# One exponential over three PSUM banks for a pair of key tiles in a graph attention

## The chip, the cores and the metric

The kernel runs on one core of a Trainium2 chip. The metric is the device time of one execution in microseconds (us); lower is better. The engines work side by side, each through its own list of instructions in order, and wait for each other through semaphores: PE multiplies matrices into PSUM (eight banks of 512 float32 columns on 128 partitions), ACT (ScalarE) computes functions such as the exponential, DVE (VectorE) and POOL (GpSimd) work element by element, SP starts DMA transfers. POOL has no part in PSUM here: what it reads lies in SBUF.

## The reference

Four graph layers are applied to 3327 nodes with 128 features, each as `x = x + layer(relu(layernorm(x)))`. The change lies in the second, an attention of 128 heads whose feature dimension per head is 8:

```python
q = (x @ Wq.T).reshape(d, n, h)          # d = 128 heads, n = 3327 nodes, h = 8
k = (x @ Wk.T).reshape(d, n, h)
v = (x @ Wv.T).reshape(d, n, h)
a = jnp.einsum('dnh,dmh->dnm', q, k) * scale
a = a + spatial_encoding + edge_encoding  # both are the adjacency matrix: + 2 * adj
a = jax.nn.softmax(a, axis=2)
out = jnp.einsum('dnm,dmh->dnh', a, v)
```

So for each head, 3327 x 3327 scores are made, twice the adjacency (0 or 2) is added to each, all are exponentiated, and the result weighs the values. The kernel takes no maximum off (another path, not run for this input, does) and gets the sum of each row from a ninth value column of ones.

## The kernel before

**Tiling.** Queries go along the columns in chunks of QW = 476 (seven chunks, the last of 471, computed as 472), keys along the partitions in T = 26 tiles of 128. Heads go in groups of four (32 groups): each head's small contraction takes one of the four 32-row groups of PE, so that four heads' score matmuls can run side by side. The loop is `steps = [(c, g, t) ...]`, chunk by chunk, group by group, key tile by key tile: 7 x 32 x 26 = 5824 steps, 2912 pairs of an even and an odd step. A pair shares one tile `p8` of eight planes of 476 columns in SBUF (`p_pool`, three buffers), four planes for each step.

**Three ways to add 2 * adj.** Each of a step's four heads has a letter in `WAYS`:

- D: PE writes the score into a PSUM tile `early` (one bank, four buffers); DVE adds `a2` (twice the adjacency) on the way to `p8` (L552). The exponential comes later.
- I: PE writes the score into a PSUM tile `late` and adds `a2` itself with a second matmul, of `two_i` (the identity) with `a2` (L550). ACT takes the exponential from PSUM to `p8` (L553).
- G: PE writes the score into `late`, ACT takes its exponential, and POOL multiplies it by `e`, the exponential of `a2` (L555).

The even step has DDDI, the odd one DDIG. `PLACES` puts the five D planes of a pair at 0 to 4, so that one ACTIVATE of 5 x 476 = 2380 columns, in place, does all of them (L557, after the odd step), and the three late ones at 5, 6 and 7:

```python
WAYS = ("DDDI", "DDIG")
PLACES = ((0, 1, 2, 5), (3, 4, 6, 7))
```

**PSUM.** `acc` takes one bank, `early` four, `late1` (even step) one, `late2` (odd step) two: all eight. `late1` and `late2` have one buffer each, so the next pair's late scores can't be written until ACT has read this pair's.

**Order.** All engines' orders are as written (`tc.manual_schedule`). `scores` issues for one step: late scores and then early scores on PE (L547), the identity matmul (L550), DVE's adds (L552), the exponential of the late tile (L553, 476 columns in the even step, 952 in the odd), POOL's multiply (L555, odd), the exponential of 2380 columns (L557, odd). After it `weigh` is called for the step `ahead = 4` steps earlier, that is two pairs: four matmuls of the values (9 columns each, on four column groups) with the planes of `p8` into `acc` (L564). They are in float32 and show in the trace as two MATMULs each. At the last key tile DVE copies `acc` out (L573) and four DMAs store it. Around these, by step number: `load_heads` loads the next group's keys, queries and values at t = 4, `key_pair` converts keys on POOL (L419) from t = 13, `Parting` splits later groups' keys and queries in the first chunk, adjacency tiles of the next chunk are loaded, doubled (L272) and stored, and in a chunk's last group ACT makes the next chunk's `e` (L347).

Of the kernel before, what the change touches and what calls it, by code (L numbers as in the profile page):

```python
# [8 lines left out]
F32 = mybir.dt.float32  # L9
# [6 lines left out]
AF = mybir.ActivationFunctionType  # L16
ALU = mybir.AluOpType
# [4 lines left out]
P = 128  # L22
N = 3327
D = 128
# [7 lines left out]
QW = 476  # L32
# [5 lines left out]
def rows_of(t):  # L38
    return P if t < T - 1 else P - 1
# [15 lines left out]
def kernel(  # L55
# [23 lines left out]
    nc = tc.nc  # L79
# [90 lines left out]
    def load_rows(dst, src, t, col0, w):  # L170

        def part(p0, p1):
            nc.sync.dma_start(dst[p0:p1, :w], dram(src, (p0 * T + t) * N + col0, [[T * N, p1 - p0], [1, w]]))

        if t < T - 1:
            part(0, P)
        else:
            part(0, 112)
            part(112, P - 1)
# [85 lines left out]
    def doubled(pool, a, t, w):  # L265
        kp = rows_of(t)
        a2 = pool.tile([P, QW], BF16, name="a2")
        if w % 2:
            nc.gpsimd.memset(a2[:, w : w + 1], 0.0)
        if kp < P:  # L270
            nc.gpsimd.memset(a2[96:P], 0.0)
        nc.gpsimd.tensor_scalar(a2[:kp, :w], a, 2.0, None, op0=ALU.mult)  # L272
        return a2
# [67 lines left out]
    def even(c):  # L341
        w = q_chunks[c][1]
        return w + w % 2

    def exp_of(a2, c):
        e = e_pool.tile([P, QW], F32, name="e")
        nc.scalar.activation(e[:, : even(c)], a2[:, : even(c)], AF.Exp)  # L347
        return e
# [65 lines left out]
    def key_pair(heads):  # L414

        k_in, _, _, pairs = heads
        t = 2 * len(pairs)
        k = kq.tile([P, 2, P], F32R, name="k", bufs=T)
        nc.gpsimd.tensor_copy(k, slots(k_in)[:, t : t + 2, :])  # L419
        pairs.append(k)  # L420

    with tc.tile_pool(name="l1", bufs=1) as pool, tc.tile_pool(name="l1_ps", bufs=3, space=PSUM) as ps:
# [21 lines left out]
        early = []  # L444
# [60 lines left out]
    WAYS = ("DDDI", "DDIG")  # L505
    PLACES = ((0, 1, 2, 5), (3, 4, 6, 7))
    two_i = const.tile([P, P], BF16, name="two_i")
# [9 lines left out]
    ahead = 4  # L517
    adj_pools.append(ctx_at.enter_context(tc.tile_pool(name="at_adj1", bufs=T)))
    with tc.tile_pool(name="at_in", bufs=1) as a_pool, tc.tile_pool(name="at_p", bufs=3) as p_pool, tc.tile_pool(
        name="at_ps", bufs=1, space=PSUM  # L520
    ) as ps:
        acc = ps.tile([P, 512], F32, name="acc")
        nc.vector.memset(acc, 0.0)

        def load_adj(c, t):

            q0, w = q_chunks[c]
            a = a_pool.tile([P, QW], F32, name="a_in", bufs=1)
            load_rows(a, adjT, t, q0, w)
            return a, t, w  # L530

        def store_adj(c, t, a2):
            q0, w = q_chunks[c]
            nc.sync.dma_start(adj16[t][:, q0 : q0 + w], a2[:, :w])

        def scores(step, heads, a2, e_a, p8):
            c, _, t = step
            we = even(c)
            _, q4, _, pairs = heads
            ways, places = WAYS[t % 2], PLACES[t % 2]  # L540
            n_d = ways.count("D")
            late = ps.tile([P, 4 - n_d, 512], F32, name=f"late{4 - n_d}")
            early = [ps.tile([P, 512], F32, name="early", bufs=4) for _ in range(n_d)]
            for i in (*range(n_d, 4), *range(n_d)):
                r = slice(32 * i, 32 * i + 32)
                sp = early[i] if i < n_d else late[:, i - n_d]
                nc.tensor.matmul(sp[:, :we], pairs[t // 2][r, t % 2, :], q4[r, :we], start=True, stop=ways[i] != "I")  # L547
            for i in range(4):
                if ways[i] == "I":
                    nc.tensor.matmul(late[:, i - n_d, :we], two_i, a2[:, :we], start=False, stop=True)  # L550
            for i in range(n_d):
                nc.vector.tensor_tensor(p8[:, places[i], :we], early[i][:, :we], a2[:, :we], op=ALU.add)  # L552
            nc.scalar.activation(p8[:, places[n_d] : places[3] + 1, :we], late[:, :, :we], AF.Exp)  # L553
            if ways[3] == "G":
                nc.gpsimd.tensor_tensor(p8[:, places[3], :we], p8[:, places[3], :we], e_a[:, :we], op=ALU.mult)  # L555
            if t % 2:
                nc.scalar.activation(p8[:, :5, :we], p8[:, :5, :we], AF.Exp)  # L557

        def weigh(step, v4, p8):
            c, g, t = step  # L560
            q0, w = q_chunks[c]
            kp = rows_of(t)
            for i in range(4):
                nc.tensor.matmul(  # L564
                    acc[32 * i : 32 * i + EA, :w],
                    v4[:kp, i, t, :],
                    p8[:kp, PLACES[t % 2][i], :w],
                    start=(t == 0),
                    stop=(t == T - 1),
                )  # L570
            if t == T - 1:
                o4 = a_pool.tile([P, QW], F32, name="o4")
                nc.vector.tensor_copy(o4[: 96 + EA, :w], acc[: 96 + EA, :w])  # L573
                for i in range(4):
                    n0 = (4 * g + i) * N + q0
                    nc.sync.dma_start(ot[:, n0 : n0 + w], o4[32 * i : 32 * i + EA, :w])

        with tc.manual_schedule(engines=engines):
            groups = [(c, g) for c in range(len(q_chunks)) for g in range(n_groups)]
            steps = [(c, g, t) for c, g in groups for t in range(T)]  # L580
            heads = first
            a_t, a_next = a_first, []
            e_t, e_next = e_first, []
            to_store = [(0, t, a2) for t, a2 in enumerate(a_t)]
            begun = {}
            for j, step in enumerate(steps):
                c, g, t = step
                n = c * n_groups + g + 1
                more = n < len(groups)
                if t == 0 and j:  # L590
                    heads = coming
                    if g == 0:
                        a_t, a_next = a_next, []
                        e_t, e_next = e_next, []
                if t % 2 == 0:
                    p8 = p_pool.tile([P, 8, QW], F32, name="p8")
                scores(step, heads, a_t[t], e_t[t // 2], p8)
                begun[j] = (step, heads[2], p8)
                if j >= ahead:
                    weigh(*begun.pop(j - ahead))  # L600
                if t == min(4, T // 2) and more:
                    coming = load_heads(*groups[n])
                if c == 0 and g + 2 < n_groups:
                    if t == 0:
                        parting = ahead_part
                    for due in range(t, t + 1 if t < T - 1 else max(T, 16)):
                        parting.at(due)
                        if due == 15 and g + 3 < n_groups:
                            ahead_part = Parting(g + 3)
                            ahead_part.load(0)  # L610
                            ahead_part.load(1)

                if t >= T // 2 and more:
                    key_pair(coming)
                if t == min(6, T // 2) and c + 1 < len(q_chunks):
                    for _ in range(min(len(to_store), 1 + T // n_groups)):
                        store_adj(*to_store.pop(0))
                    a_in = [load_adj(c + 1, i) for i in range(len(a_next), T * (g + 1) // n_groups)]
                if t == max(T - 4, 3) and c + 1 < len(q_chunks):
                    for a, i, w in a_in:  # L620
                        a_next.append(doubled(adj_pools[(c + 1) % 2], a[: rows_of(i), :w], i, w))
                        to_store.append((c + 1, i, a_next[-1]))
                if t % 2 and g == n_groups - 1 and c + 1 < len(q_chunks):
                    e_next.append(exp_of(a_next[t], c + 1))
            for j in range(len(steps) - ahead, len(steps)):
                weigh(*begun.pop(j))
            for a in to_store:
                store_adj(*a)
# [372 lines left out]
    with tc.For_i(0, n_once, 1):  # L1001
# [5 lines left out]
        with tc.tile_pool(name="sh", bufs=2) as pool, tc.tile_pool(name="sh_ps", bufs=2, space=PSUM) as ps:  # L1007
            with tc.For_i(0, NH, 1) as hd:
# [5 lines left out]
                for t in range(T):  # L1014
# [4 lines left out]
                    for half, (h0, hw) in enumerate(chunks(N, 2048)):  # L1019
                        sp = ps.tile([P, 2048], F32, name="sp")  # L1020
# [9 lines left out]
        with tc.tile_pool(name="gb", bufs=2) as pool, tc.tile_pool(name="gb_ps", bufs=2, space=PSUM) as ps, tc.tile_pool(  # L1030
            name="gb_acc", bufs=1, space=PSUM
# [3 lines left out]
            with tc.For_i(0, NH // 4, 1) as g:  # L1035
# [8 lines left out]
                for q0, w in chunks(N, QW):  # L1044
                    q4 = pool.tile([P, QW], F32, name="gq4")
                    for i in range(4):
                        nc.sync.dma_start(q4[32 * i : 32 * i + EA, :w], qf[:, bass.ds(g * (4 * N) + i * N + q0, w)])
                    for t in range(T):
# [4 lines left out]
                        for i in range(4):  # L1053
                            r = slice(32 * i, 32 * i + EA)
                            sp = ps.tile([P, 512], F32, name="gsp")
# [3 lines left out]
                        for i in range(4):  # L1059
                            r = slice(32 * i, 32 * i + EA)  # L1060
# [49 lines left out]
```

## Time and profile before

| | us |
|---|---|
| median of 3 runs | 11191.26 (11190.45 to 11191.84) |
| profiled execution | 11195.14 |
| its span on the core | 11193.4 |
| PE busy, of the stretch 580 to 10480 us | 9781.47 of 9900 |
| ACT busy, same stretch | 9891.59 |
| DVE busy, same stretch | 8530.47 |
| POOL busy, same stretch | 5812.99 |

The stretch from 580 to 10480 us is the attention; the granted PE clock in it is 1.00. The page's groups read: line, engine, operation, output<-inputs with partitions x elements and type, count | total busy us, mean ns of one | idle time of the engine just before them, and what ended most of it. "(+1 forms)" means that instructions of another shape are in the same group: L553 mixes 476 and 952 columns. Records of one engine can overlap, since the next instruction begins while the last one's results are on their way; PE's records start at the true time, but their ends are modelled. In the timeline each row is a start, the time from the first start to the last end of the instructions merged in it, engine, line, operation, count, and in brackets the idle time before and what ended it. PEld are weight loads.

### The profile page before, as it was taken

The numbers are of one execution on the slowest core, as the hardware profiler recorded it, in microseconds if no ns is written. First come the engines' busy times: TensorE is split into PE (matmuls) and PEld (weight loads), VectorE is DVE, ScalarE is ACT, GpSimd is POOL, SyncE is SP. The second block draws the span as 40 slices with busy tenths as digits, with TensorE's granted clock in tenths as the row PEclk, the third lists the DMA queues.
The fourth block names the chain that finished last, engine by engine and source line by source line (L and its number), as shares of the span: only waits on it lengthen the run. The fifth ranks groups of instructions, "written<-read, shape, count | busy, mean of one in ns | idle before, by whom it ended". The sixth has DMA issues, their size and how long they took to land. (4 is left out here: it accounts for less than half of the span.)

```text
span 11193.4 us, 209350 instructions
## 1 busy us (share of the span) xinstructions
PE 10850.5 (97%) x79530; PEld 3005.9 (27%) x79530; DVE 9343.1 (83%) x15429; ACT 10199.3 (91%) x9152; POOL 6016.3 (54%) x6964
## 2 busy tenths in 40 slices
PE   9899999999999999999999999999999999999996
PEld 4322222222222222222222222222222222222453
DVE  8588888888888888888888888888888888888656
ACT  0399999999999999999999999999999999999522
POOL 0277777555555555555555555555555555555203
PEclk9899999999999999999999999999999999999998
DMA  7755554333333333333333333333333332333432
GB/s 264 238 129 120 123 127 109 65 64 64 68 64 62 67 66 63 68 65 61 68 66 63 66 66 61 67 66 61 66 66 61 66 63 55 61 58 58 135 113 97
DMA packets 417541, 942.25 MB, mean 84 GB/s; under 512 B 67936, under 2 KB 345937, under 8 KB 380940
## 3 DMA queue, kind: packets, MB, share of 16 engines
q1 hardware_dynamic: 412762, 918.98, 37.4%
q8 instruction: 627, 10.27, 0.4%
q0 software_dynamic: 3760, 9.78, 0.3%
q14 instruction: 392, 3.21, 0.1%
HBM read 788.78 MB, written 139.71 MB: 83 GB/s over the span
## 5 line engine op out<-in xcount | busy, mean ns | idle before, releaser
L552 DVE TENSOR_TENSOR p<-early,a 128x476 f32<-128x476 f32 (+1 forms) x14560 | 8426.4, 646 | 1369.4 <-PE early L547 1297.5
L557 ACT ACTIVATE p<-p 128x2380 f32<-128x2380 f32 (+1 forms) x2912 | 7568.4, 2599 | 0.4
L564 PE MATMUL acc<-p,v 128*9 128x476 f32 (+1 forms) x46592 | 5748.5, 564 | 15.3 <-ACT p L557 1.4
L553 ACT ACTIVATE p<-late 128x476 f32<-128x476 f32 (+1 forms) x5824 | 5315.4, 1175 | 13.8 <-DMA q<-qt 10.2
L555 POOL TENSOR_TENSOR p<-p,e 128x476 f32<-128x476 f32 (+1 forms) x2912 | 3528.1, 1212 | 3204.3 <-ACT p L553 2998.6
L547 PE MATMUL late<-q,k 32*128 32x476 f32 (+1 forms) x8736 | 2798.2, 478 | 99.5 <-ACT p L553 39.7
L547 PE MATMUL early<-q,k 32*128 32x476 f32 (+1 forms) x14560 | 2843.6, 478 | 9.4 <-DVE p L552 9.4
L419 POOL CAST k<-k_in 128x256 fp32r<-128x256 f32 x2912 | 1936.5, 697 | 886.4 <-DMA k_in<-kt 339.4
L547 PEld LDWEIGHTS late<-q,k 32*128 32x128 f32 x8736 | 1065.4, 181 | 4890.4 <-ACT p L553 4186.2
L550 PE MATMUL late<-a,two_i 128*128 128x476 bf16 (+1 forms) x5824 | 2180.8, 374 | 0.0
L547 PEld LDWEIGHTS early<-q,k 32*128 32x128 f32 x14560 | 1113.0, 181 | 9.9 <-DVE p L552 9.9
L564 PEld LDWEIGHTS acc<-p,v 128*9 128x9 f32 x46592 | 695.2, 88 | 1272.6 <-issue 1185.8
L550 PEld LDWEIGHTS <-two_i 128*128 128x128 bf16 x5824 | 556.2, 96 | 1329.0 <-issue 1329.0
L189 ACT COPY agg<-agg_ps 128x512 f32<-128x512 f32 x15 | 8.2, 591 | 485.5 <-PE agg_ps L204 290.6
L230 PE MATMUL agg_ps<-a,part 128*128 128x512 bf16 (+1 forms) x1092 | 227.0, 369 | 4.3 <-ACT agg L928 3.2
L272 POOL TENSOR_SCALAR a<-a_in 128x476 bf16<-128x476 f32 (+2 forms) x156 | 221.1, 1417 | 0.5
L272 POOL TENSOR_SCALAR a<-a 128x476 bf16<-128x476 f32 (+1 forms) x26 | 36.4, 1400 | 288.1 <-DMA a<-in_adjT_dram 288.1
L923 PE MATMUL sp<-yT,hT 128*128 128x512 f32 (+1 forms) x364 | 170.7, 610 | 12.3 <-ACT agg L928 6.4
L204 PE MATMUL agg_ps<-a,h 128*128 128x512 f32 (+2 forms) x364 | 148.2, 570 | 26.2 <-DVE h L164 26.2
L573 DVE COPY o<-acc 105x476 f32<-105x476 f32 (+1 forms) x224 | 144.5, 645 | 4.6 <-PE acc L564 4.6
L204 PE MATMUL agg_ps<-a,x 128*128 128x512 f32 (+2 forms) x364 | 145.3, 562 | 0.6 <-ACT x L318 0.6
L230 PEld LDWEIGHTS <-part 128*128 128x128 f16 x1092 | 108.6, 99 | 117.7 <-issue 10.3
(236 smaller groups left out, 2592.0 us busy)
## 6 DMA issues: line engine op xcount, KB each, us to landing
k_in<-kt SPq DMA_DIRECT2D x1792, 207.9 KB
v<-vd SPq DMA_DIRECT2D x896, 117.0 KB
a<-in_adjT_dram SPq DMA_DIRECT2D x50, 1663.5 KB
a<-adj SPq DMA_DIRECT2D x78, 831.8 KB
q<-qt SPq DMA_DIRECT2D x1536, 29.8 KB
a_in<-in_adjT_dram SPq DMA_DIRECT2D x125, 238.0 KB
adj<-a SPq DMA_DIRECT2D x156, 119.0 KB
vd<-v_st SPq DMA_DIRECT2D x25, 576.0 KB
```

The lines of the kernel that those rows point to most:

```text
L204: nc.tensor.matmul(acc[c][:, :w], lhs[:kp, t, :], a[:kp, c0 : c0 + w], start=(t == 0), stop=(t == T - 1))
L230: nc.tensor.matmul(acc[c][:, :w], part[:, t, :], a[:, c0 : c0 + w], start=(t == 0 and i == 0), stop=(t == T - 1 and i == len(parts) - 1),)
L272: nc.gpsimd.tensor_scalar(a2[:kp, :w], a, 2.0, None, op0=ALU.mult)
L419: nc.gpsimd.tensor_copy(k, slots(k_in)[:, t : t + 2, :])
L547: nc.tensor.matmul(sp[:, :we], pairs[t // 2][r, t % 2, :], q4[r, :we], start=True, stop=ways[i] != "I")
L550: nc.tensor.matmul(late[:, i - n_d, :we], two_i, a2[:, :we], start=False, stop=True)
L552: nc.vector.tensor_tensor(p8[:, places[i], :we], early[i][:, :we], a2[:, :we], op=ALU.add)
L553: nc.scalar.activation(p8[:, places[n_d] : places[3] + 1, :we], late[:, :, :we], AF.Exp)
L555: nc.gpsimd.tensor_tensor(p8[:, places[3], :we], p8[:, places[3], :we], e_a[:, :we], op=ALU.mult)
L557: nc.scalar.activation(p8[:, :5, :we], p8[:, :5, :we], AF.Exp)
L564: nc.tensor.matmul(acc[32 * i : 32 * i + EA, :w], v4[:kp, i, t, :], p8[:kp, PLACES[t % 2][i], :w], start=(t == 0), stop=(t == T - 1),)
L923: nc.tensor.matmul(sp[:, c0 : c0 + w], slots(zT)[:, t, :], z2T[:, cols], start=True, stop=False)
```

## The change

`scores` is now called once a pair, at the even step, with both steps' `a2`. The two late tiles become one tile `late` of three neighbouring banks. PE gets: the even step's three early tiles, the three late scores (heads 3, 2 and 3 of the steps, so the last two use row groups that the first four matmuls already use), both identity matmuls, and then the odd step's two early tiles. ACT gets one exponential of 3 x 476 = 1428 columns in place of one of 476 and one of 952, and right after it the 2380 columns. POOL's multiply becomes `times_e`, issued at the odd step. `weigh` is called at odd steps for two steps at once, those of two pairs earlier. The work on each plane, its place in `p8` and the number of buffers stay.

```diff
-        def scores(step, heads, a2, e_a, p8):
+        def scores(step, heads, a2s):
+
             c, _, t = step
             we = even(c)
             _, q4, _, pairs = heads
-            ways, places = WAYS[t % 2], PLACES[t % 2]
-            n_d = ways.count("D")
-            late = ps.tile([P, 4 - n_d, 512], F32, name=f"late{4 - n_d}")
-            early = [ps.tile([P, 512], F32, name="early", bufs=4) for _ in range(n_d)]
-            for i in (*range(n_d, 4), *range(n_d)):
+            p8 = p_pool.tile([P, 8, QW], F32, name="p8")
+            late = ps.tile([P, 3, 512], F32, name="late")
+
+            def score(odd, i, sp):
                 r = slice(32 * i, 32 * i + 32)
-                sp = early[i] if i < n_d else late[:, i - n_d]
-                nc.tensor.matmul(sp[:, :we], pairs[t // 2][r, t % 2, :], q4[r, :we], start=True, stop=ways[i] != "I")
-            for i in range(4):
-                if ways[i] == "I":
-                    nc.tensor.matmul(late[:, i - n_d, :we], two_i, a2[:, :we], start=False, stop=True)
-            for i in range(n_d):
-                nc.vector.tensor_tensor(p8[:, places[i], :we], early[i][:, :we], a2[:, :we], op=ALU.add)
-            nc.scalar.activation(p8[:, places[n_d] : places[3] + 1, :we], late[:, :, :we], AF.Exp)
-            if ways[3] == "G":
-                nc.gpsimd.tensor_tensor(p8[:, places[3], :we], p8[:, places[3], :we], e_a[:, :we], op=ALU.mult)
-            if t % 2:
-                nc.scalar.activation(p8[:, :5, :we], p8[:, :5, :we], AF.Exp)
+                nc.tensor.matmul(sp[:, :we], pairs[t // 2][r, odd, :], q4[r, :we], start=True, stop=WAYS[odd][i] != "I")
+
+            def early(odd):
+                for i in range(WAYS[odd].count("D")):
+                    sp = ps.tile([P, 512], F32, name="early", bufs=4)
+                    score(odd, i, sp)
+                    nc.vector.tensor_tensor(p8[:, PLACES[odd][i], :we], sp[:, :we], a2s[odd][:, :we], op=ALU.add)
+
+            early(0)
+            lates = [(odd, i) for odd in range(2) for i in range(4) if WAYS[odd][i] != "D"]
+            for n, (odd, i) in enumerate(lates):
+                assert PLACES[odd][i] == 5 + n
+                score(odd, i, late[:, n])
+            for n, (odd, i) in enumerate(lates):
+                if WAYS[odd][i] == "I":
+                    nc.tensor.matmul(late[:, n, :we], two_i, a2s[odd][:, :we], start=False, stop=True)
+            early(1)
+            nc.scalar.activation(p8[:, 5:, :we], late[:, :, :we], AF.Exp)
+            nc.scalar.activation(p8[:, :5, :we], p8[:, :5, :we], AF.Exp)
+            return p8
+
+        def times_e(step, p8, e_a):
+            we = even(step[0])
+            assert WAYS[1][3] == "G"
+            nc.gpsimd.tensor_tensor(p8[:, PLACES[1][3], :we], p8[:, PLACES[1][3], :we], e_a[:, :we], op=ALU.mult)
...
                 if t % 2 == 0:
-                    p8 = p_pool.tile([P, 8, QW], F32, name="p8")
-                scores(step, heads, a_t[t], e_t[t // 2], p8)
+                    p8 = scores(step, heads, a_t[t : t + 2])
+                else:
+                    times_e(step, p8, e_t[t // 2])
                 begun[j] = (step, heads[2], p8)
-                if j >= ahead:
-                    weigh(*begun.pop(j - ahead))
+                if t % 2:
+                    for i in (j - 1 - ahead, j - ahead):
+                        if i >= 0:
+                            weigh(*begun.pop(i))
```

## The prediction

> **What bounds the kernel now.** I read the page first: busy times, then the costliest groups, all of them in one stage, the attention.
>
> ```profile
> PE 10850.5 (97%) x79530; PEld 3005.9 (27%) x79530; DVE 9343.1 (83%) x15429; ACT 10199.3 (91%) x9152; POOL 6016.3 (54%) x6964
> ...
> L557 ACT ACTIVATE p<-p 128x2380 f32<-128x2380 f32 (+1 forms) x2912 | 7568.4, 2599 | 0.4
> ...
> L553 ACT ACTIVATE p<-late 128x476 f32<-128x476 f32 (+1 forms) x5824 | 5315.4, 1175 | 13.8 <-DMA q<-qt 10.2
> ```
>
> PE, ACT and DVE are all close to full, so no share settles it. ACT's records overlap (7568 + 5315 is more than the stage lasts), so its idle column can't show a wait. The period of a pair must come from starts. The first and the last L557, from the timeline of ACT at both ends of the stage:
>
> ```profile
> 579.10 2.19 ACT L557 ACTIVATE p<-p 128x2380 f32<-128x2380 f32 x1
> ...
> 10470.58 2.66 ACT L557 ACTIVATE p<-p 128x2360 f32<-128x2360 f32 x1
> ```
>
> 9891.5 us over 2911 intervals is 3.398 us a pair. In steady stretches it is 3.37: here the timeline of all engines, one pair and a bit.
>
> ```profile
> 7002.00 1.39 ACT L553 ACTIVATE p<-late 128x952 f32<-128x952 f32 x1
> ...
> 7002.59 0.18 PEld L547 LDWEIGHTS late<-q,k 32*128 32x128 f32 x1 [0.87 <-ACT p L553]
> 7002.59 0.48 PE L547 MATMUL late<-q,k 32*128 32x476 f32 x1
> ...
> 7002.85 2.63 ACT L557 ACTIVATE p<-p 128x2380 f32<-128x2380 f32 x1
> ...
> 7003.02 0.37 PE L550 MATMUL late<-a,two_i 128*128 128x476 bf16 x1
> 7003.25 2.90 DVE L552 TENSOR_TENSOR p<-early,a 128x476 f32<-128x476 f32 x5 [0.47 <-PE early L547]
> 7003.32 0.12 PEld L564 LDWEIGHTS acc<-p,v 128*9 128x9 f32 x8 [0.21 <-issue]
> 7003.32 0.98 PE L564 MATMUL acc<-p,v 128*9 128x476 f32 x8
> ...
> 7004.23 0.48 PE L547 MATMUL late<-q,k 32*128 32x476 f32 x2
> ...
> 7004.93 1.86 ACT L553 ACTIVATE p<-late 128x476 f32<-128x476 f32 x2
> ...
> 7006.22 2.64 ACT L557 ACTIVATE p<-p 128x2380 f32<-128x2380 f32 x1
> ```
>
> ACT's first small exponential starts at 7001.55 (the timeline of ACT alone), so its starts go 0.45 (476 columns), 0.85 (952), 2.08 (2380): 3.37 in all, back to back. One column costs 0.40/476 us (0.85 - 0.45 over 476 more), so an ACTIVATE has some 0.05 of its own, the big one 0.08. PE needs .43 (scores) + .30 (identity) + .91 (weighing), 1.64 a step, 3.28 a pair, and waits 0.09 for ACT in front of the late tile. DVE works 2.90 of 3.37.
>
> A second bound lies as close, a loop over two pairs: late tile (7002.59) to first add 0.66, five adds 2.90, 0.03 to L557 (the least distance I find in the trace), 2.08 to the next small exponential, its record of 0.98, 0.05 until PE takes up the bank (7002.54 to 7002.59). 6.70 for two pairs, 3.35 each. ACT's rate and this loop are 0.02 apart.
>
> **Part by part.** *One exponential instead of two.* 2912 ACTIVATEs go at 0.05: ACT's own rate becomes 3.37 - 0.05 = 3.32, at most 148 us of gain. The column count is the same.
>
> The Trainium skill would price it higher: "ScalarE: Activation LUTs", What ACT_TABLE_LOAD costs, gives an ACTIVATE 186 ns beside its columns, of which back-to-back ones overlap by about 93. By it the gain on ACT would be 2912 x 0.093 = 271 us, an estimate; the starts above show 0.05.
>
> *Order on PE.* All counts stay: per pair 8 score, 2 identity, 8 weighing matmuls (16 passes). But the order becomes: three early tiles and late tile 0, late 1 and 2, both identities, two early tiles, all weighing. The second step's four score tiles, which ran side by side on four row groups, are now cut in two by the identities. What each piece costs:
>
> ```profile
> 621.61 0.45 PE L547 MATMUL early<-q,k 32*128 32x476 f32 x1
> 621.99 0.38 PE L550 MATMUL late<-a,two_i 128*128 128x476 bf16 x1
> ...
> 102.14 2.31 PE L204 MATMUL agg_ps<-a,h 128*128 128x512 f32 x5
> ...
> 10601.77 1.03 PE L230 MATMUL agg_ps<-a,part 128*128 128x512 bf16 x4
> ```
>
> A lone last score tile takes 0.38 until the identity starts (first two lines, cut from the timeline so that only it is seen), four together 0.42. Two identities in a row I price at 0.20, from L230: four matmuls of 512 columns, starts 0.22 apart, with new weights each, times 476/512. Identity to the next kind: 0.30 (7003.02 to 7003.32). The same reason gives 0.20 for the second batch on row groups already in use: its weights load behind the running batch, as L204's do (0.43 apart for 512 columns, a load of 0.19 in each). The bounds are 0.20 and 0.38, a lone batch paid in full; 0.20 is nearest, since nothing but the tile changes. Two early tiles to weighing: 0.38, at most 0.42. One step's weighing takes 0.91 until score tiles follow (7003.32 to 7004.23), and 0.81 where more weighing follows (less the same 0.10 by which 0.30 exceeds 0.20): both steps together 1.72.
>
> From late tile 0 to the next pair's first early tile PE needs .38 + .20 + .20 + .30 + .38 + 1.72 = 3.18; its own period, with four tiles in front (+.04), is 3.22, under ACT's 3.32.
>
> A rule of the Trainium skill speaks against this order. "TensorE: Matmul & The Clock Gate", Part 3, The mechanism, says that weight loads overlap running matmuls only where the row group differs (or a background buffer takes them). By Part 2 of that page 128 columns load in 128/1.2 = 107 ns, so a second batch would cost 0.11 more and the sum below some 100 us, an estimate. The L204 row shows loads hidden on the same rows, though in full-array mode.
>
> *The wait.* PE's late tile 0 waits for the exponential that reads the one three-bank tile. Before, two tiles gave two waits, one for each. Behind it in PE's queue stand the identities, the last two early tiles, 16 passes of weighing, and then the next pair's first three early tiles. DVE waits for those, L557 for DVE's five adds, and the next three-bank exponential stands behind L557 on ACT. So the loop now is: late tile of pair n, PE 3.18, early tiles of pair n+1 to the first add 0.66, five adds 2.90, 0.03, L557 of n+1 to the three-bank exponential of n+2 2.08, its record 1.39 + 0.40 = 1.79, 0.05, late tile of n+3. That is 10.69 over three pairs, **3.563 a pair**. The old loop had no PE leg, since each pair's early tiles stood beside its late tile; now a late tile and weighing stand between them.
>
> *Costed at nothing.* The multiply by e keeps its place among POOL's instructions, and DVE's, POOL's and SP's sequences (the DMAs too) are the same in the built program. It starts when the three-bank exponential ends (at late tile n+1) and has until the weighing of pair n, one period and .58 + .20 + .30 + .38 later: 1.21 of work in 5.0. Without that cover PE's weighing would wait for it. Three p buffers still suffice: weighing of pair n-2 stands before the early tiles of n+1, as before, and ends with them.
>
> *Sum.* 3.563 - 3.371 = 0.192, times 2912 = +559. Beside the steady period, before has 0.027 a pair (79 us) at group ends and for the 91 exponentials of L347 on ACT (0.49 each, 45 us). In a loop that passes each such place once in three pairs I count a third: -53. Together **+506** on the profiled 11195.1 us (span 11193.4): 11701. The median of the runs is 3.9 lower, so **11697**.
>
> Bounds: an identity that needs no switch (0.20 for 0.30) lowers the period by 0.033, -97. A second batch at 0.38, early tiles at 0.42 and a second identity at 0.30 raise it by 0.18 + 0.04 + 0.10 over three, +311. The forecast's own range is 11600 to 11800.
>
> **Rivals.** *ACT's rate decides* (faster): if the loop has slack that I don't see, the period is 3.32 and the time 11191 - 148 = 11043. For it: before sits on ACT's rate to 0.02. Against it: it decides only if the loop is under 9.96 (3 x 3.32), 0.73 shorter than its sum, and all terms but PE's unseen ones (at most 0.10 shorter) are read from rows that reproduce 3.35 before. Another order of waits could do it. 9%.
>
> *PE is longer* (slower): if every unseen PE term is at its high end, the loop is 3.67 and the time about 12010; from a second batch of 0.31 on it leaves the forecast's own range. The split of score tiles on the same row groups is shown nowhere. 13%.
>
> *Nothing moves*: PE's fewer mode switches and ACT's 0.05 pay for the loop, 11191 within 22. The loop would have to be 3.37, 0.58 under its sum. 4%.
>
> That the change doesn't do what it says is out: the built program has one 1428-column exponential a pair.
>
> **Numbers.** The forecast has 74%. The range 11580 to 11900 takes the forecast and the nearer part of the longer PE, and leaves out about 2 in 10. Differences under 0.2% (22 us) can't be told from none: faster 0.09, same 0.04, slower 0.87.
>
> **What would show it.** Right: the period of L564 starts (the old L557) near 3.56; ACT with true gaps before it, released by DVE, some 0.24 a pair; PE waiting about 0.3 at the late tile, released by ACT; DVE waiting for early tiles for 0.66 a pair. A lone-tile batch visible between the identities and the weighing. Wrong: starts at 3.32 with no gap on ACT (the first rival), or no wait of PE at the late tile and a period that is PE's own work (the second). The sum rests on the PE leg of 3.18 and on in-order queues; if late tiles start without waiting for ACT, it falls.

## The result, and the profile after

| | before | after |
|---|---|---|
| median of 4 runs, us | 11191.55 (11190.45 to 11194.51) | 11387.28 (11386.82 to 11390.15) |
| profiled execution, us | 11195.14 | 11386.82 |
| its span, us | 11193.4 | 11385.1 |

The ratio is 1.0175, with a 95% interval of 1.0157 to 1.0193: slower, by some 196 us. The prediction had the direction and 2.6 times the amount (+506); 11387 lies under its range.

The page of the kernel after: engines, the chain of waits, and the groups that answer to those shown before.

```profile
PE 11166.0 (98%) x79530; PEld 3885.4 (34%) x79530; DVE 9352.5 (82%) x15429; ACT 10333.4 (91%) x6240; POOL 6018.1 (53%) x6964
...
PE 90%; ACT 3%; issue 3%; DVE 1%; DMA 1%; POOL 1%; SPq 0%; ACTq 0%; DVEq 0%; POOLq 0%
...
L564 ACT ACTIVATE p<-p 128x2380 f32<-128x2380 f32 (+1 forms) x2912 | 6372.8, 2188 | 63.3 <-DVE p L552 13.1
...
L563 ACT ACTIVATE p<-late 128x1428 f32<-128x1428 f32 (+1 forms) x2912 | 3909.3, 1342 | 10.5 <-DMA k_in<-kt 10.0
L546 PEld LDWEIGHTS early<-q,k 32*128 32x128 f32 x14560 | 1276.4, 181 | 3482.7 <-DVE p L552 3154.6
```

Two things are new. L564, the exponential of 2380 columns, has 2188 ns a record where L557 had 2599 for the same work. And the idle time of PE's weight loads now stands in front of the early tiles, 3483 us, most of it ended by DVE's adds; before, it stood in front of the late tiles, 4890 us, most of it ended by ACT. Its size is no measure of a stall, for runs below in which PE waits less have as much (3503 us in e6, 3475 in e8). PE's share of 98% and its 90% of the chain say little: its records have modelled ends and fill a wait that lies inside them.

The first and the last L564, from the timeline of ACT at both ends of the stage:

```profile
577.93 2.19 ACT L564 ACTIVATE p<-p 128x2380 f32<-128x2380 f32 x1 [1.53 <-DVE p L552]
...
10663.92 2.17 ACT L564 ACTIVATE p<-p 128x2360 f32<-128x2360 f32 x1
```

That is 10086.0 us over 2911 intervals, 3.465 a pair against 3.398 before; 0.067 x 2911 = 194, the whole of the loss (the spans differ by 192). In steady stretches a pair takes 3.446 (median) against 3.371. One such pair, in the timeline of all engines:

```profile
7002.33 0.48 PE L546 MATMUL early<-q,k 32*128 32x476 f32 x3
7002.44 2.19 ACT L564 ACTIVATE p<-p 128x2380 f32<-128x2380 f32 x1
...
7002.47 0.69 PE L546 MATMUL late<-q,k 32*128 32x476 f32 x3
...
7002.94 2.89 DVE L552 TENSOR_TENSOR p<-early,a 128x476 f32<-128x476 f32 x5 [0.54 <-PE early L546]
...
7003.10 0.57 PE L561 MATMUL late<-a,two_i 128*128 128x476 bf16 x2
7003.60 0.23 PEld L546 LDWEIGHTS early<-q,k 32*128 32x128 f32 x2 [0.39 <-DVE p L552]
...
7004.06 1.79 PE L577 MATMUL acc<-p,v 128*9 128x476 f32 x16
...
7004.53 1.34 ACT L563 ACTIVATE p<-late 128x1428 f32<-128x1428 f32 x1
...
7005.77 0.48 PE L546 MATMUL early<-q,k 32*128 32x476 f32 x3
...
7005.87 2.19 ACT L564 ACTIVATE p<-p 128x2380 f32<-128x2380 f32 x1
```

Early tiles to early tiles: 7002.33 to 7005.77, 3.44. Two rows hidden in merged lines, cut from the timelines of DVE and of PE by short windows:

```profile
7002.94 0.65 DVE L552 TENSOR_TENSOR p<-early,a 128x476 f32<-128x476 f32 x1 [0.54 <-PE early L546]
...
7003.65 0.48 PE L546 MATMUL early<-q,k 32*128 32x476 f32 x1
```

The first of the five adds runs from 7002.94 to 7003.59. The second row is the pair's fifth early tile, at 7003.65, just behind that add's end and 0.05 behind the fourth (7003.60). There are four `early` banks: the fifth tile takes the bank of the first, which the first add has to read out. This is no accident of one pair: from the 5th to the 95th percentile of all 2912 pairs, the fifth tile starts 0.054 to 0.055 after the first add's end. Two closed loops can be read from these lines.

- *Over three pairs*, the prediction's: late tile 7002.47 to the next early tiles 7005.77, 3.30; first add 0.61 behind them; five adds 2.89; 0.04; L564 to L563 2.09; L563's record 1.34; 0.06 to the next late tile (7005.87 to 7005.93). Sum 10.33, or 3.443 a pair.
- *Over one pair*, which the prediction doesn't have; I call it the bank loop: early tiles to first add 0.61, the add 0.65, 0.06 to the fifth tile, 0.41 to the weighing, 1.71 of weighing, next early tiles. Sum 3.44.

ACT's own work is 3.32, so it has gaps of some 0.12 a pair. Both loops give the measured period (3.446) within 0.01, so the trace alone doesn't tell which decides, nor whether the old kernel stood at the edge of a loop at all. That is what the experiments are for.

### The profile page after: what moved, and what is told of

Same layout as the page of the kernel before. It is cut to its first block, busy times and chain, and to the rows that moved or that the text cites. A ratio compares the mean times of both kernels' runs of the same rounds, so it can differ in the third digit from the quotient of the medians.

```text
span 11385.1 us, 206439 instructions
## 1 busy us (share of the span) xinstructions
PE 11166.0 (98%) x79530; PEld 3885.4 (34%) x79530; DVE 9352.5 (82%) x15429; ACT 10333.4 (91%) x6240; POOL 6018.1 (53%) x6964
## 4 chain that ended last, share of the span: by engine, by line
PE 90%; ACT 3%; issue 3%; DVE 1%; DMA 1%; POOL 1%; SPq 0%; ACTq 0%; DVEq 0%; POOLq 0%
PE acc L577 42%; PE early L546 22%; PE late L561 12%; PE late L546 8%; PE agg_ps L204 2%; ACT p L563 1%; ACT p L564 1%; PE agg_ps L230 1%; PE pp L464 1%; PE yp L754 0%; DMA k_in<-kt 0%; POOL rows L970 0%; ACT e L347 0%; PE pp L471 0%; PE mp L315 0%
## 5 line engine op out<-in xcount | busy, mean ns | idle before, releaser
L564 ACT ACTIVATE p<-p 128x2380 f32<-128x2380 f32 (+1 forms) x2912 | 6372.8, 2188 | 63.3 <-DVE p L552 13.1
L577 PE MATMUL acc<-p,v 128*9 128x476 f32 (+1 forms) x46592 | 5191.0, 563 | 0.7 <-ACT p L564 0.7
L563 ACT ACTIVATE p<-late 128x1428 f32<-128x1428 f32 (+1 forms) x2912 | 3909.3, 1342 | 10.5 <-DMA k_in<-kt 10.0
L546 PE MATMUL early<-q,k 32*128 32x476 f32 (+1 forms) x14560 | 3017.8, 478 | 10.2 <-DVE p L552 9.0
L546 PEld LDWEIGHTS early<-q,k 32*128 32x128 f32 x14560 | 1276.4, 181 | 3482.7 <-DVE p L552 3154.6
L546 PE MATMUL late<-q,k 32*128 32x476 f32 (+1 forms) x8736 | 2022.3, 409 | 5.7
L577 PEld LDWEIGHTS acc<-p,v 128*9 128x9 f32 x46592 | 994.6, 90 | 2338.0 <-issue 2332.8
L561 PE MATMUL late<-a,two_i 128*128 128x476 bf16 (+1 forms) x5824 | 1674.6, 369 | 0.0
L546 PEld LDWEIGHTS late<-q,k 32*128 32x128 f32 x8736 | 852.3, 183 | 29.2 <-ACT p L563 29.2
L561 PEld LDWEIGHTS <-two_i 128*128 128x128 bf16 x5824 | 330.6, 97 | 965.8 <-issue 965.8
L230 PE MATMUL agg_ps<-a,part 128*128 128x512 bf16 (+1 forms) x1092 | 243.4, 379 | 47.7 <-issue 43.1
L204 PE MATMUL agg_ps<-a,h 128*128 128x512 f32 (+2 forms) x364 | 147.1, 567 | 26.4 <-DVE h L164 26.4
L230 PEld LDWEIGHTS <-part 128*128 128x128 f16 x1092 | 109.7, 101 | 176.4 <-issue 75.1
L204 PE MATMUL agg_ps<-a,x 128*128 128x512 f32 (+2 forms) x364 | 145.3, 562 | 0.6 <-ACT x L318 0.6
```

Source lines behind the costliest of these rows:

```text
L204: nc.tensor.matmul(acc[c][:, :w], lhs[:kp, t, :], a[:kp, c0 : c0 + w], start=(t == 0), stop=(t == T - 1))
L230: nc.tensor.matmul(acc[c][:, :w], part[:, t, :], a[:, c0 : c0 + w], start=(t == 0 and i == 0), stop=(t == T - 1 and i == len(parts) - 1),)
L546: nc.tensor.matmul(sp[:, :we], pairs[t // 2][r, odd, :], q4[r, :we], start=True, stop=WAYS[odd][i] != "I")
L561: nc.tensor.matmul(late[:, n, :we], two_i, a2s[odd][:, :we], start=False, stop=True)
L563: nc.scalar.activation(p8[:, 5:, :we], late[:, :, :we], AF.Exp)
L577: nc.tensor.matmul(acc[32 * i : 32 * i + EA, :w], v4[:kp, i, t, :], p8[:kp, PLACES[t % 2][i], :w], start=(t == 0), stop=(t == T - 1),)
```

## The experiments

Each ratio is to the median of the kernel before on the same chip: 11195.77 for e1 to e4, 11186.78 for e5 to e8, 11189.74 for e9 and e10. Each was run two or four times, e10 ten times. "Steady" is the median distance between starts of the 2380-column exponential.

### A known cost inside the three-pair loop: e1 and e2

The first question was whether a loop through DVE's adds and L564 decides, and over how many pairs. An operation that changes nothing (the maximum of a plane with itself) lengthens DVE's work in front of L564. Its own record is 0.69 on average, but instructions of DVE start 0.56 apart, and 0.56 is what it holds the exponential back by. A loop over k pairs so gains 0.56/k. In the kernel after:

```diff
             early(1)
             nc.scalar.activation(p8[:, 5:, :we], late[:, :, :we], AF.Exp)
+            nc.vector.tensor_tensor(p8[:, 3, :we], p8[:, 3, :we], p8[:, 3, :we], op=ALU.max)
             nc.scalar.activation(p8[:, :5, :we], p8[:, :5, :we], AF.Exp)
```

> The changed kernel with one more DVE instruction a pair (plane 3 of p8 becomes the maximum of itself with itself, after the fifth add), some 0.56 us like its neighbours. Theory loop (one loop over three pairs: late tile, PE 3.30, next early tiles to first add 0.61, five adds 2.90, 0.03, L564 to L563 2.10, L563 1.34, 0.05; 10.33, 3.443 a pair): 0.56/3 = 0.187 a pair, 545 us more than the changed kernel, some 11930. Theory PE (the split score batch makes PE's own work 3.44 a pair, DVE has slack of 0.54 a pair): within 60 us of 11387. A loop over two pairs instead of three: 0.28 a pair, some 12200.

Measured: 12008.29, ratio 1.0725 [1.0704, 1.0746], 78 us over the loop theory's 11930. One pair of the timeline shows the delay, from the first add to the 2380-column exponential (here L565):

```profile
7001.36 2.90 DVE L552 TENSOR_TENSOR p<-early,a 128x476 f32<-128x476 f32 x5
...
7004.86 2.19 ACT L565 ACTIVATE p<-p 128x2380 f32<-128x2380 f32 x1
```

That is 3.50, against 2.93 in the kernel after (7002.94 to 7005.87). The mean period is 3.678, 0.213 above that of the kernel after: nearest to a third of 0.56 (0.187), away from half of it (0.28), from all of it and from nothing. The timeline of ACT in this kernel:

```profile
7030.61 2.19 ACT L565 ACTIVATE p<-p 128x2380 f32<-128x2380 f32 x1
...
7034.52 2.19 ACT L565 ACTIVATE p<-p 128x2380 f32<-128x2380 f32 x1 [0.47 <-DVE p L564]
...
7038.02 2.19 ACT L565 ACTIVATE p<-p 128x2380 f32<-128x2380 f32 x1
...
7041.47 2.19 ACT L565 ACTIVATE p<-p 128x2380 f32<-128x2380 f32 x1
```

The starts are 3.91, 3.50 and 3.45 apart, 10.86 in all, where the loop of 10.33 with 0.56 more is 10.89: one pair in three pays. A loop over three pairs has one chain of work for three pairs, and this is how it looks. What the mean has beyond a third lies in single pairs: the eighth of a group, where POOL converts keys, takes 4.20 in the median.

A rival is that DVE, with six instructions a pair, has become the bound by its own work. Its line on this page:

```profile
L552 DVE TENSOR_TENSOR p<-early,a 128x476 f32<-128x476 f32 (+1 forms) x14560 | 8442.7, 645 | 446.3 <-PE early L546 399.9
```

DVE is close to full, but it still waits 446 us for PE's early tiles, 0.15 a pair, so it doesn't set the period alone. The loop of the prediction exists, and over the right number of pairs.

The same operation in the kernel before asks whether that one was also at the edge of a loop, as the prediction said (3.35 beside ACT's 3.37):

```diff
                 nc.vector.tensor_tensor(p8[:, places[i], :we], early[i][:, :we], a2[:, :we], op=ALU.add)
+            if t % 2:
+                nc.vector.tensor_tensor(p8[:, 3, :we], p8[:, 3, :we], p8[:, 3, :we], op=ALU.max)
```

> The kernel before with the same additional DVE instruction of 0.56 us a pair. Theory A (records of the saturated ACT are longer than the work: 0.98 shown for 476 columns where 0.40 + 0.15 = 0.55 is work; the loop before is 6.26 over two pairs, 3.13, with 0.24 a pair of slack under ACT's 3.37): (6.26 + 0.56)/2 = 3.41, 0.04 a pair more, some 11300 and at most 11450 with group ends. Theory B (the records are true, as the prediction had it: the loop is 6.70): 3.63 a pair, 0.26 more, some 11950.

Measured: 11678.9, 1.0431 [1.041, 1.0452]. As a total it lies between the two theories and bears out neither. By pair it is clearer: in quiet stretches the period is 3.38 to 3.45, 3.41 on average, where a two-pair loop of 6.70 would need (6.70 + 0.56)/2 = 3.63 in every pair. Two such periods, 6.82, leave at most 6.26 for the loop without the added 0.56, or 3.13 a pair. So the old loop had slack, some 0.24 a pair under ACT's 3.37. The rest of the loss is in the second pair of a group (3.93 in the median) and in pairs in which POOL converts keys (3.45 to 3.71). Neither theory had named where it comes from, DVE's own work. On this kernel's page DVE is busy for 11133 us of the span of 11675, and its adds wait hardly at all:

```profile
L552 DVE TENSOR_TENSOR p<-early,a 128x476 f32<-128x476 f32 (+1 forms) x14560 | 8410.3, 643 | 64.1 <-PE early L547 38.5
```

Six starts 0.56 apart are 3.36 a pair, and a seventh, the copy of `acc` that comes once a group, makes it 3.92. While POOL converts keys, the maximum itself is slower: its record is 863 ns on average beside a conversion and 681 otherwise (799 and 652 in e1), and the adds keep their 0.56. So with a sixth instruction DVE is the bound in most of this kernel. The same page has a line that matters more for the prediction, the small exponentials:

```profile
L555 ACT ACTIVATE p<-late 128x476 f32<-128x476 f32 (+1 forms) x5824 | 4095.6, 757 | 17.6 <-DMA vd<-v_st 10.1
```

757 ns on average where the kernel before has 1175 (L553). The work is the same. The difference is that ACT was the bound before and isn't here. The prediction took such a long record, 0.98, as a leg of a loop, and 1.39 for the new kernel.

### Order or merged tile: e3 and e9

e3 keeps the new order on PE and divides the late tile and its exponential in two again:

```diff
-            late = ps.tile([P, 3, 512], F32, name="late")
+            late1 = ps.tile([P, 1, 512], F32, name="late1")
+            late2 = ps.tile([P, 2, 512], F32, name="late2")
+            late = [late1[:, 0], late2[:, 0], late2[:, 1]]
...
-            nc.scalar.activation(p8[:, 5:, :we], late[:, :, :we], AF.Exp)
+            nc.scalar.activation(p8[:, 5:6, :we], late1[:, :, :we], AF.Exp)
+            nc.scalar.activation(p8[:, 6:, :we], late2[:, :, :we], AF.Exp)
```

> The changed kernel's order on PE, but with two late tiles (one bank, two banks) and two exponentials of 476 and 952 columns. Theory loop: ACT's part of the loop is late tile 1 released after 0.45 + 0.95 in place of 1.34, PE's part begins 0.1 earlier or later; ACT has slack, so one more instruction of 0.05 costs at most 0.1/3: 3.41 to 3.48 a pair, 11300 to 11450; the order on PE and not the merged tile makes the loss. Theory merge (the single buffer of three banks is what costs): back at 3.37, 11191 within 40.

Measured: 11394.09, 1.0176 [1.0156, 1.0197], steady 3.448. The loss is there without the merged tile. On its page, the three exponentials:

```profile
L567 ACT ACTIVATE p<-p 128x2380 f32<-128x2380 f32 (+1 forms) x2912 | 6378.6, 2190 | 22.8 <-DVE p L554 9.8
...
L566 ACT ACTIVATE p<-late 128x952 f32<-128x952 f32 (+1 forms) x2912 | 2790.2, 958 | 0.0
...
L565 ACT ACTIVATE p<-late 128x476 f32<-128x476 f32 (+1 forms) x2912 | 1605.6, 551 | 10.4 <-DMA vd<-v_st 9.9
```

The two small ones take 0.55 and 0.96 here, 0.98 and 1.39 in the kernel before, the big one 2.19 and 2.6. In the kernel before they start 0.45, 0.85 and 2.08 apart although their records are 0.4 longer, so the longer record is no longer work. It is read here as waiting on a full ACT; the runs show when it comes and goes, not what it consists of.

e9 does the opposite: the order of before, one three-bank tile for the pair, and one exponential of it in the odd step.

```diff
-            late = ps.tile([P, 4 - n_d, 512], F32, name=f"late{4 - n_d}")
+            if t % 2 == 0:
+                lates[0] = ps.tile([P, 3, 512], F32, name="late")
+            late = lates[0][:, t % 2 : 1 + 2 * (t % 2)]
...
-            nc.scalar.activation(p8[:, places[n_d] : places[3] + 1, :we], late[:, :, :we], AF.Exp)
+            if t % 2:
+                nc.scalar.activation(p8[:, 5:, :we], lates[0][:, :, :we], AF.Exp)
```

> The kernel before, its order on PE and its calls step by step unchanged, with the three late scores in one three-bank tile and one exponential of 1428 columns at the odd step. Theory: the merged tile closes a loop in each pair, from late tile 0 over the even step (0.42 + 0.30 + 0.91), the odd step's scores (0.42), its identity's record and the start of ACT (0.37 + 0.13), the exponential's 1.34 and 0.05: 3.94 a pair for 3.37, some 12850; the order of the change is what makes the merge bearable. Rival (the merge is worth ACT's 0.05 by itself): 11040.

Measured: 12907.73, 1.1535 [1.1512, 1.1558]. Its timeline shows a loop of one pair between PE and ACT alone:

```profile
7031.24 1.36 ACT L558 ACTIVATE p<-late 128x1428 f32<-128x1428 f32 x1 [0.53 <-PE late L554]
...
7032.65 0.48 PE L551 MATMUL late<-q,k 32*128 32x476 f32 x1 [0.62 <-ACT p L558]
...
7034.29 0.48 PE L551 MATMUL late<-q,k 32*128 32x476 f32 x2
...
7035.20 1.36 ACT L558 ACTIVATE p<-late 128x1428 f32<-128x1428 f32 x1 [0.52 <-PE late L554]
```

The even step's late tile waits for the exponential of the pair before (end of its record 7032.60), the odd step's late tiles stand a weighing behind it (7034.29), and the next exponential needs those: 3.96 a pair. In the old order the merged tile costs 1718 us; in the new order the loss is there with and without it.

### What closes the loop in the kernel after: e4

If the three-pair loop decides, it can be cut by ACT's order: L564 of a pair is held back until L563 of the next pair is issued, so that L563 no longer stands behind an L564 that waits for DVE.

```diff
             nc.scalar.activation(p8[:, 5:, :we], late[:, :, :we], AF.Exp)
-            nc.scalar.activation(p8[:, :5, :we], p8[:, :5, :we], AF.Exp)
+            if held:
+                held.pop()()
+            held.append(lambda: nc.scalar.activation(p8[:, :5, :we], p8[:, :5, :we], AF.Exp))
```

> The changed kernel with L563 of pair n+1 issued on ACT before L564 of pair n, so that a late tile's release no longer stands behind DVE's adds of its own pair. Theory loop: the loop over three pairs is cut; what is left is ACT's rate of 3.32 to 3.37 and PE's own 3.30: 3.34 a pair, 11100 to 11230. Theory PE (PE's own work is 3.44): 11387 within 40. A third way: weighing of pair n now waits for the later L564, and the time rises over 11450.

Measured: 11387.05, 1.017 [1.0153, 1.0187], steady 3.448. A miss for the loop theory: nothing moved, the number being that of the kernel after to a fraction of a microsecond. Either PE's own work is the bound, or a second loop of the same length stands beside the first. The timeline of e4, with two rows cut out by short windows at the end:

```profile
7002.57 0.49 PE L548 MATMUL early<-q,k 32*128 32x476 f32 x3
...
7003.20 0.58 PE L563 MATMUL late<-a,two_i 128*128 128x476 bf16 x2
...
7003.71 0.65 PE L548 MATMUL early<-q,k 32*128 32x476 f32 x2
...
7004.29 1.78 PE L581 MATMUL acc<-p,v 128*9 128x476 f32 x16
...
7006.01 0.48 PE L548 MATMUL early<-q,k 32*128 32x476 f32 x3
...
7003.18 0.65 DVE L554 TENSOR_TENSOR p<-early,a 128x476 f32<-128x476 f32 x1 [0.54 <-POOL p L574]
...
7003.89 0.47 PE L548 MATMUL early<-q,k 32*128 32x476 f32 x1
```

The two last early tiles are merged in one line, but the second of them starts at 7003.89, 0.18 behind the first, where tiles on different row groups otherwise start 0.01 apart. The first add ends at 7003.83. (Its row names a multiply of POOL, which by the program's order belongs to the pair before and to another `p8`; the first add of the next pair names PE at the same distance.) Here the bank wait is plain: early tiles to first add 0.61, add 0.65, 0.06, 0.40 to the weighing, 1.72, again 3.44. It was found only because this run missed.

### Two tests of the bank loop: e5 and e6, e7 and e8

*Shorten it.* The first add of a pair is also the first writer of its `p8` and has to wait until the earlier users of that buffer are done, as well as for PE. A memset of two columns of another plane (overwritten later), issued to DVE ahead of the pair's tiles, takes those waits while DVE is idle anyway:

```diff
+            nc.vector.memset(p8[:, 7, 0:2], 0.0)
             early(0)
```

That is e5, on the kernel after; e6 has it and e4's order on ACT.

> The changed kernel with a DVE memset of two columns of p8's plane 7 in front of each pair's first add: it takes the waits for p8's release (PE, ACT, POOL) in DVE's idle time, so that the first add waits for its score tile alone and starts some 0.09 earlier (0.52 after the early tiles' start for 0.61). Theory bank (one loop in each pair: early tiles to first add 0.61, the add 0.65, 0.05 until PE takes its bank for the fifth early tile, 0.41 to weighing, 1.72 to the next early tiles; 3.44): this loop falls to 3.35, the loop over three pairs (10.29 without the wait for the bank) to 10.20, 3.40 a pair: 11260 within 40. Theory PE (its own work is 3.44): 11387 within 30.

> The same memset in the kernel where L563 of pair n+1 stands before L564 of pair n. Theory bank: the loop over three pairs is cut, the bank's loop is 3.35, ACT's rate 3.32 to 3.37, PE's own work 3.25: 3.36 a pair, 11100 to 11180. Theory PE: 11387 within 30.

Measured: e5 11264.6, 1.0067 [1.0051, 1.0084]; e6 **11132.61, 0.9951 [0.9935, 0.9968]**, faster than both kernels. Of e5 the starts of its 2380-column exponential, from ACT's timeline:

```profile
7045.78 2.19 ACT L565 ACTIVATE p<-p 128x2380 f32<-128x2380 f32 x1
...
7049.14 2.19 ACT L565 ACTIVATE p<-p 128x2380 f32<-128x2380 f32 x1
...
7052.63 2.19 ACT L565 ACTIVATE p<-p 128x2380 f32<-128x2380 f32 x1
...
7055.98 2.19 ACT L565 ACTIVATE p<-p 128x2380 f32<-128x2380 f32 x1
```

3.36, 3.49, 3.35, and so on: the bank loop is down to 3.35, and now the three-pair loop shows, again as one long pair in three. In e6, where ACT's order cuts that one too, the timeline of all engines has

```profile
7033.00 0.48 PE L548 MATMUL early<-q,k 32*128 32x476 f32 x3
...
7033.24 0.06 DVE L556 MEMSET p<- 128x2 f32 x1 [0.18 <-issue]
...
7033.51 2.89 DVE L554 TENSOR_TENSOR p<-early,a 128x476 f32<-128x476 f32 x5 [0.21 <-PE early L548]
...
7034.63 1.78 PE L582 MATMUL acc<-p,v 128*9 128x476 f32 x16
...
7036.35 0.49 PE L548 MATMUL early<-q,k 32*128 32x476 f32 x3
```

The first add comes 0.51 behind the early tiles (0.61 in e4), the weighing 1.63 (1.72), the next early tiles 3.35 (3.44). All of the gain in steady pairs (3.448 to 3.349) is the 0.1 ahead of the first add, in every pair, so the add stands in a loop of one pair.

*Take it away.* Without the odd step's second early score matmul there are four tiles for four banks, and the fifth add reads the fourth tile again. Head 1 of each odd key tile so gets head 0's scores, and PE has one matmul less. e7 does so with e4's order on ACT, e8 on the kernel after:

```diff
                 for i in range(WAYS[odd].count("D")):
-                    sp = ps.tile([P, 512], F32, name="early", bufs=4)
-                    score(odd, i, sp)
+                    if not (odd and i):
+                        sp = ps.tile([P, 512], F32, name="early", bufs=4)
+                        score(odd, i, sp)
                     nc.vector.tensor_tensor(p8[:, PLACES[odd][i], :we], sp[:, :we], a2s[odd][:, :we], op=ALU.add)
```

> The kernel with the two exponentials swapped, without the score matmul of the odd step's second early tile (head 1); DVE's fifth add reads the fourth tile again, so that head 1 of odd key tiles gets head 0's scores. Four early tiles a pair on four banks: no tile waits for the first add of its own pair. Two tiles side by side take PE as long as one. Theory bank: what is left is ACT's 3.32 to 3.37: 3.34 a pair, 11040 to 11150. Theory PE: 11387 within 40.

> The changed kernel without the score matmul of the odd step's second early tile, DVE's fifth add reading the fourth tile again. Theory two loops (the bank's and the one over three pairs lie 0.01 apart): the second stays with 10.29/3 = 3.43 a pair, 11340 within 30. Theory bank alone: 3.34 as in the swapped kernel, 11100. Theory PE: 11387.

Measured: e7 11033.66, 0.9863 [0.9843, 0.9882], steady 3.321, 6 us under the range of the bank theory; e8 11325.98, 1.0124 [1.0104, 1.0144], with medians of 3.450, 3.447 and 3.336 by turns. In e8 the three-pair loop remains and sets 3.41 on average. In e7 neither loop is left, and the timeline of ACT shows an engine that is the bound again:

```profile
7031.13 2.29 ACT L569 ACTIVATE p<-p 128x2380 f32<-128x2380 f32 x1
7033.21 1.47 ACT L566 ACTIVATE p<-late 128x1428 f32<-128x1428 f32 x1
7034.46 2.30 ACT L569 ACTIVATE p<-p 128x2380 f32<-128x2380 f32 x1
```

Starts 2.08 and 1.25 apart, 3.33 here and 3.321 in the median, records longer than that again, though by 0.1 and not by the 0.4 of the kernel before. PE's own work was not what held e4 at 3.448: it fits into 3.349 with all its matmuls (e6, steady).

### Is the memset a gain by itself: e10

The same memset in the kernel before, where ACT decides:

```diff
+            if t % 2 == 0:
+                nc.vector.memset(p8[:, 5, 0:2], 0.0)
             for i in range(n_d):
                 nc.vector.tensor_tensor(p8[:, places[i], :we], early[i][:, :we], a2[:, :we], op=ALU.add)
```

> The kernel before with a DVE memset of two columns of p8's plane 5 in front of each pair's first add, as in the changed kernel's variant (there plane 7). Theory: before is set by ACT's own 3.37, and DVE's loop has 0.24 a pair of slack, so nothing moves: 11187 within 25. If the earlier first add helps here too, the gain of the swapped variant would have been had without the change: under 11150.

Measured over 10 runs: 11187.88, 0.9998 [0.9988, 1.0007]. Nothing moves, though the first add does come earlier: 0.55 behind the first early tile in the median of all pairs, 0.65 in the kernel before. The 0.1 is worth something only where the first add lies on a loop that decides.

## Why the prediction was right or wrong

**"Two waits become one ... So the loop now is": right in kind.** The loop was named with its places and its three pairs; e1 shows that it is there and that a cost in it counts a third. e3 shows that the order on PE closes it, as "The old loop had no PE leg" says.

**"Its record 1.39 + 0.40 = 1.79": the term that failed.** L563's record is 1.34. The 1.39 (952 columns) came from an ACT that was the bound, where records are longer; where ACT has gaps, the same instruction takes 0.96 (e3), so 0.96 + 0.40 = 1.36 would have been near. The prediction itself gave the new kernel gaps on ACT of 0.24 a pair, which doesn't go with a record taken from a full ACT. 0.45 over three pairs is 0.15 a pair, 437 us of the 506.

**"ACT's rate and this loop are 0.02 apart": wrong, by the same term.** With 0.55 in place of 0.98, the old loop of 6.70 is 6.27, 3.14 a pair, 0.24 under ACT's rate. That the sum came out at 3.35 wasn't a confirmation: the 0.98 had been stretched by the rate that the sum was compared with. e2 shows the slack in its quiet pairs; its total is set by DVE's own work.

**"From late tile 0 to the next pair's first early tiles PE needs 3.18": 3.30.** By the rows above: 0.63 to the identities (priced 0.58), 0.50 for both and the switch (0.50), 0.46 to the weighing (0.38, and 0.05 of the difference is the bank wait), 1.71 (1.72). The bank wait itself was missed: the prediction checked the three `p8` buffers under the new order, but not the four `early` ones, whose fifth tile now stands before a weighing instead of behind one. It put this wait at nothing without saying so. In the kernel before, the odd step's tiles came 1.64 after the even step's (7002.59, 7004.23), 0.33 after the first add's end (begun 0.66 after them, 0.65 long).

**The second batch on busy row groups.** In e4, where no late tile waits for ACT, early tiles to identity take 7002.57 to 7003.20, 0.63, where one batch of four took 0.43 (7002.59 to 7003.02): a net cost of 0.20, as priced. That price is L230's spacing; L204, on which it leaned for hidden loads, doesn't show them, since its 0.43 between starts is as much as L230's 0.22 and its own load of 0.19 in a row (an estimate). The Trainium skill ("TensorE: Matmul & The Clock Gate", Part 3, The mechanism) would, by the prediction's reading, have had the second load outside, 0.31 in all, an estimate; the net cost in e4 shows no such extra. The page also names a background buffer as an exception, and no run here tells whether it was used.

**"One exponential instead of two", 0.05 a pair: right.** With both loops out of the way (e7) the period is 3.321 = 3.371 - 0.05. The 0.093 of "ScalarE: Activation LUTs" (What ACT_TABLE_LOAD costs) would make it 3.278, an estimate; e7 does not show that.

**The sum.** +506 by the prediction. The loop is 10.33 instead of 10.69: record -0.45, PE leg +0.12, first add -0.05, other legs +0.02, so -0.12 a pair, -349 us. What the loop leaves beside the steady pairs (group ends and the like) is 0.019 a pair (3.465 - 3.446), not the 0.009 that "I count a third" gave: +29. The rest, 0.003 a pair or 9 us, is less than the rows can resolve. 506 - 349 + 29 + 9 = 195, against 196 measured; that it closes to 1 us is luck. With the right record alone the sum would have been +69; with a PE leg of 3.25 too (3.30 without the bank wait) some +137. That would have been within 60 us without the bank loop, because the two loops lie 0.01 apart, and right for half of the reason, as e4 shows.

**The rivals.** "ACT's rate decides" gave 11043: e7, a kernel that leaves a score matmul out and has ACT's order changed, comes to 11034 with both loops gone. "PE is longer" priced a PE leg of up to 3.50; it measured 3.30, and e6, with all of PE's work in the new order, has a period of 3.349. What was to be seen in the profile came out smaller throughout: ACT's gaps 0.12 (0.24 expected) and released by DVE, PE's wait in front of the late tile 0.14 (0.3 expected; 7002.33 to 7002.47), DVE's wait 0.54 (0.66).

## What to carry to other kernels

- The length of a record on an engine that is itself the bound is not the length of the work: take legs of a loop from where the engine has gaps, or from distances between starts, or the engine's rate is counted twice.
- When the order of tiles changes, go round each ring of buffers with the new order: five tiles on four banks were harmless while a weighing stood between the first and the fifth, and a loop of one pair when it stood behind.
- A known cost put into a suspected loop tells how many rounds it spans, by the share of it that a round pays; and when cutting one loop moves nothing, look for a second of equal length. With one cut and the other shortened (e6: ACT's two exponentials in the other order, and a two-column memset that takes the buffer's waits early) the one-piece order runs at 0.9951 of the kernel before.

## What the runs showed of the hardware

- An ACTIVATE's record can grow when ACT is saturated, for the same work: 0.55 in e3 to 0.98 before (476 columns), 0.96 to 1.39 (952), 2.19 to 2.6 (2380), while starts in the saturated kernel are 0.45, 0.85 and 2.08 apart. How far it grows isn't settled: e10 has 2.65 for the 2380 columns, but e7, with ACT the bound too, 2.27 on average. The growth takes time: in the kernel before, the first L557 of the stage has 2.19, as quoted in the prediction, and one at 7002.85 has 2.63. A consumer waits for the long record's end: PE's late tile began 0.05 after it (7002.54 to 7002.59) and POOL's multiply 0.08 after the 952 columns' (7003.39 to 7003.47). So the result is truly late, but not for the work's sake.
- The first writer of a buffer with several earlier users paid about 0.1 beside what it visibly waits for: from the early tiles to the first add 0.61 falls to 0.51 (e4, e6), and 0.65 to 0.55 (before, e10), when another instruction takes the waits first. Which of the waits costs it was not separated.
